# A Mamba and local-attention kernel: dt\*x\*B on GpSimd, scan states in PSUM, a fifth matmul bank, and P times V in one stretch

## The chip, the cores and the metric

The kernel runs on one core of a Trainium2 chip. The metric is the device time of one execution in microseconds. A core has TensorE (PE in the profile; its weight loads are listed as PEld), VectorE (DVE), ScalarE (ACT), GpSimd (POOL) and SyncE (SP), which here only issues DMAs. Each engine works through its own queue in order, and engines wait for each other through semaphores.

## The reference

The input x has 4096 tokens of 256 features. It is normalized once, and two independent branches work on the result:

```python
xn = _layernorm(x)
x  = x + mamba(xn) + local_transformer(xn)
```

The Mamba branch has 512 channels and 16 states per channel. After an input projection, a causal convolution of 4 taps and a silu, it computes dt, B and C for each token and runs the recurrence

```python
dA  = exp(dt * A)                 # per channel and state
h   = dA * h + (dt * x_conv) * B  # along the 4096 tokens
y   = sum over states of h * C
out = (y + x_conv * D) * silu(z) @ out_proj
```

The transformer branch has two layers. Each has 8 heads of 64, with normalized and rotated queries and keys, a softmax over a window of 128 tokens and the window before it, an output projection, and a gated MLP with 682 hidden units. All arithmetic is float32.

## The kernel before, in words

The transformer branch is cut into 16 steps of 256 tokens per layer, so 32 steps `(l, s)`; each step has two attention windows of 128 tokens. The Mamba branch is cut into 8 blocks of 512 tokens, each with 4 groups of 128 channels (`c`). The two branches run interleaved over the whole execution.

The order of the work is not written by hand. Functions such as `project`, `attend`, `mlp`, `prepare` and `recur` only record pieces of work with `add(engine, us, emit, reads, writes, soon=...)`. `Plan.order` (L175 to L281) then lays them out: it keeps a planned time for each engine, takes from the pieces that are ready and whose buffers are free the one with the smallest key, and emits all pieces in the order of their planned starts. The key is the step in which the piece was recorded less its `soon`; `AHEAD` (L43) limits how far ahead of the oldest open piece the plan looks. The numbers `us` and `soon` so decide each engine's queue, and the chip then runs the queues as they stand. A buffer (`buffer(name, n, shape)`) has n tiles that pieces of work take in turn; a new value can be written when all readers of the old one are done.

PSUM has 8 banks of 512 floats per partition. They are: four matmul banks `mm` (L320), one for `dtx` (L321), two for the decays `da` (L322) and one for the sums `y` (L323).

**The recurrence** (`recur`, L709 to L768). For each block, channel group and pair of states `g` (8 pairs): SP loads B and C of the pair, spread over all partitions, into two `bc` tiles (L718 to L723). VectorE multiplies dt\*x (in PSUM, `dtx`) by B into `u` (L726, 128x1024). For each of the two states ScalarE writes the decay exp(dt\*A) into a `da` bank (L734) and VectorE runs the scan along the 512 tokens, reading `da` and `u` and writing the states over `u` (L739). ScalarE copies the last column of both states for the next block (L745). GpSimd multiplies `u` by C (L748, 128x1024), and in every second pair also adds the two states (L753). TensorE adds the result to `y` by transposing matmuls (L757), 4 for an added pair and 8 otherwise. `close` (L770) copies `y` out, transposes it back (L778) and multiplies by the gate.

**The attention** (`project` L836, `attend` L924). TensorE projects q, k, v (L846); ScalarE squares and VectorE reduces for the norms (L857, L859), VectorE and GpSimd rotate (L891, L893, L906, L913, L873), TensorE transposes (L878) and ScalarE copies to `qT`, `kT` (L884). In `attend` each window has two groups `g` of four heads. The scores (L945) use half of the array's rows, 64 x 128. VectorE masks and takes the maximum (L960), ScalarE takes exponentials and divides (L970, L981). TensorE transposes P for two heads at a time (L993), ScalarE copies it to `prT` (L997), and TensorE multiplies it by V (L1005), with half of the array's columns, 128 x 64. Transposing and P times V are recorded separately for each of the two head pairs of a group, the copy between them. `project_out` (L1019, L1028) follows, and `mlp` (L1045) with its up products (L1092) and down products (L1158, L1177).

Each of these products takes a bank of `mm`, which is free again when VectorE or ScalarE has read it out. The float32 matmuls appear as two records each in the profile, the transposes as one.

Of the kernel before, what the change touches and what calls it, by code (L numbers as in the profile page):

```python
# [27 lines left out]
P = 128  # L28
# [3 lines left out]
TB = 512  # L32
# [10 lines left out]
AHEAD = 2.960000  # L43
# [78 lines left out]
class Work:  # L122


    def __init__(self, engine, us, emit, key, late, port):
        self.engine, self.us, self.emit, self.key, self.late, self.port = engine, us, emit, key, late, port
        self.before, self.after, self.values = {}, [], []
        self.n_before = 0
        self.ready = self.start = self.end = 0.0


class Plan:
# [17 lines left out]
    def add(self, engine, us, emit, reads=(), writes=(), late=0.0, port=False, holds=(), soon=0.0):  # L150
# [4 lines left out]
        w = Work(engine, us, emit, self.key - soon, late, port)  # L155
# [19 lines left out]
    def order(self):  # L175
# [3 lines left out]
        port = {"DVE": 0.0, "POOL": 0.0}  # L179
        rank = {w: i for i, w in enumerate(self.works)}  # L180
# [15 lines left out]
        while len(done) < len(self.works):  # L196
# [23 lines left out]
            while open_[e]:  # L220
# [14 lines left out]
                if w.port and e == "DVE" and port["POOL"] > now and chosen is None:  # L235

                    later.append((k, r, w))
                    if len(later) < 4:
                        continue
                    break  # L240
                chosen = w
# [9 lines left out]
            if e == "POOL":  # L251
                start = max(start, port["DVE"])
            elif w.port:
                start = max(start, port["POOL"])
            w.start, w.end = start, start + w.us + self.TAIL[e] + w.late
# [33 lines left out]
def mamba_and_local_transformer(  # L289
# [30 lines left out]
    banks = buffer("mm", 4, [P, 512], psum, True)  # L320
    dtxs_b = buffer("dtx", 1, [P, TB], psum)  # L321
# [9 lines left out]
    queries = buffer("qT", 3, [P, HP, P])  # L331
# [3 lines left out]
    probs_T = buffer("prT", 2, [P, 2, 2, P])  # L335
    heads_T = buffer("OT", 3, [P, HP, P])
# [12 lines left out]
    dts_b = buffer("dt", 2, [P, TB])  # L349
    spreads = buffer("bc", 3, [P, NG, TB])  # L350
# [73 lines left out]
    def dma(kb, to, of, reads=(), writes=(), soon=0.0):  # L424

        add("SP", 0.1, lambda: nc.sync.dma_start(to(), of()), reads, writes, late=2.2 + kb / 170.0, soon=soon)

    def load_qkv(l):
        for s in range(3):
            cut = slice(s * INNER, (s + 1) * INNER)  # L430
            dma(
                512, lambda cut=cut: wqkv.ap[:, :, cut],
                lambda cut=cut: wqkv_d[l][:, cut].rearrange("(k p) n -> p k n", p=P), writes=[(wqkv, s)], soon=-0.85,
            )

    def load_rest(l):
        dma(512, lambda: wo.ap, lambda: wo_d[l].rearrange("(h p) n -> p h n", p=P), writes=[wo], soon=-0.09)
        for half in range(2):
            for m, n in ((0, WHOLE), (NM - 1, LAST)):
# [4 lines left out]
                    writes=[(w1, (half, m))], soon=0.84,  # L444
# [4 lines left out]
            lambda: w2_d[l][0:whole, :].rearrange("(m p) n -> p m n", p=MC), writes=[(w2, 0)], soon=0.33,  # L449
        )  # L450
        dma(112, lambda: w2.ap[0 : HID - whole, NM - 1, :], lambda: w2_d[l][whole:HID, :], writes=[(w2, 1)], soon=1.13)
# [28 lines left out]
        add("PE", 5.3, shift, [w1], [pb], soon=0.05)  # L480
        add("DVE", 0.4, bias, [pb], [b1, b1x])
        add("DVE", 3.2, scale, [], [w1], port=True, soon=-0.08)
# [14 lines left out]
    def base_of(s):  # L497

        base = plan.value(rows_b)
        if s in sums:  # L500
            dma(256, lambda: base.ap, lambda: sums[s].ap, [sums[s]], [base], soon=-1.36)
            return base
        dma(256, lambda: base.ap, lambda: rows(x, s), writes=[base], soon=-1.5)
# [3 lines left out]
            ), [], [base], soon=0.03,  # L507
# [3 lines left out]
    def finish(s, po, base):  # L511

        add("DVE", 0.6, lambda: nc.vector.tensor_tensor(base.ap, halves(po), base.ap, ALU.add), [po], [base], soon=0.27)
        if s in sums:
            dma(256, lambda: rows(out, s), lambda: base.ap, [base], soon=-0.74)
            return
        sums[s] = plan.fixed(dram.tile([P, NW, D], F32, tag=f"sum{s}", name=f"sum{s}"))
        dma(256, lambda: sums[s].ap, lambda: base.ap, [base], [sums[s]], soon=0.48)
# [4 lines left out]
    def shift_column(l, s):  # L523
        now = xts[l, s]
        if s == 0:
            add("POOL", 0.14, lambda: nc.gpsimd.memset(now.ap[:, 1, 0:1], 0.0), [], [(now, 0)], soon=-0.2)
        else:
# [3 lines left out]
                [(old, 1)], [(now, 0)], soon=-0.25,  # L531
            )

    def normalize(s):

        xb, mv, rstd, pt = (plan.value(b) for b in (rows_b, small["mv"], small["rstd"], banks))
        dma(256, lambda: xb.ap, lambda: rows(x, s), writes=[xb], soon=-0.52)
# [26 lines left out]
        add("DVE", 1.1, stats, [xb], [mv], soon=-0.26)  # L564
        add("ACT", 0.5, root, [mv], [rstd], soon=-0.43)
        add("DVE", 0.6, centre, [mv, rstd], [xb], port=True, soon=-0.43)
        now = xts[0, s] = plan.value(tokens)
        add("PE", 0.44, turn, [xb], [pt], holds=[now], soon=-0.59)
        add("ACT", 0.48, lambda: nc.scalar.copy(now.ap[:, :, 1:], halves(pt)), [pt], [(now, 1)], soon=-0.67)
        shift_column(0, s)  # L570
        dma(256, lambda: xn_d[s].ap, lambda: now.ap[:, :, 1:], [(now, 1)], [xn_d[s]], soon=0.02)
# [3 lines left out]
    def reload(s):  # L575
        now = xts[1, s] = plan.value(tokens)
        dma(256, lambda: now.ap[:, :, 1:], lambda: x1_d[s].ap, [x1_d[s]], [(now, 1)], soon=0.49)
# [6 lines left out]
    def in_half(i):  # L584
# [3 lines left out]
            lambda: in_wT[:, i * DI : (i + 1) * DI].rearrange("(k p) n -> p k n", p=P), writes=[w], soon=0.21,  # L588
# [3 lines left out]
    def in_proj(b, w, c, to):  # L592
# [9 lines left out]
        add("PE", 1.72, emit, [w, xms[b]], [pm], holds=[to], soon=0.01)  # L602
        return pm

    def front_load(b):
        xm = xms[b] = plan.value(xms_b)
        for i in range(PB):
            s = b * PB + i
            dma(
                256, lambda i=i: xm.ap[:, :, i * TS : (i + 1) * TS], lambda s=s: xn_d[s].ap, [xn_d[s]], [(xm, i)], soon=0.24  # L610
# [5 lines left out]
    def front_conv(b, c, w):  # L616
        xin, xc, tail = plan.value(rows_m), xcs[b], tails[b]
        edge = slice(c * (TAPS - 1), (c + 1) * (TAPS - 1))
        if b == 0:
            add("POOL", 0.14, lambda: nc.gpsimd.memset(xin.ap[:, 0 : TAPS - 1], 0.0), [], [(xin, 0)], soon=-0.78)  # L620
        else:
# [3 lines left out]
                [(old, c)], [(xin, 0)], soon=-0.2,  # L625
            )
        pm = in_proj(b, w, c, xin)
        add("ACT", 0.48, lambda: nc.scalar.copy(xin.ap[:, TAPS - 1 :], pm.ap), [pm], [(xin, 1)], soon=-0.08)
        if b < NB - 1:
            add(  # L630
                "POOL", 0.14, lambda: nc.gpsimd.tensor_copy(tail.ap[:, edge], xin.ap[:, TB:]), [(xin, 1)], [(tail, c)], soon=0.1
            )
# [4 lines left out]
            ), [], [pm], soon=0.55,  # L637
# [8 lines left out]
        for j in range(TAPS - 1):  # L646
            add("DVE", 0.7, lambda j=j: tap(j), [xin, pm], [(xc, c) if j == TAPS - 2 else pm], soon=0.07)
# [8 lines left out]
    def front_dbl(b):  # L656
# [7 lines left out]
        add("PE", 3.43, emit, [xc], [px], holds=[xd], soon=0.14)  # L664
        add("ACT", 0.48, lambda: nc.scalar.copy(xd.ap, px.ap[0:n]), [px], [xd], soon=0.63)
        xds[b] = xd
        bc = bcs[b] = plan.fixed(dram.tile([2 * NS, TB], F32, tag=f"bc{b}", name=f"bc{b}"))
        dma(64, lambda: bc.ap, lambda: xd.ap[DTR:, :], [xd], [bc], soon=-0.06)

    def gate_conv(b, c, w):  # L670
# [4 lines left out]
        add("ACT", 0.48, lambda: nc.scalar.copy(sz.ap[:, c, :], pz.ap), [pz], [(sz, c)], soon=-1.07)  # L675

    def prepare(b, c):
# [5 lines left out]
            "PE", 1.05, lambda: nc.tensor.matmul(  # L683
                pd.ap, lhsT=dtw[:, c * P : (c + 1) * P], rhs=xd.ap[0:DTR, :], start=True, stop=True
            ), [xd], [pd], holds=[dt, e], soon=0.18,
# [3 lines left out]
        add("ACT", 0.59, lambda: nc.scalar.activation(e.ap[:, n], pd.ap, AF.Abs, bias=col("dt_b", c)), [pd], [e], soon=-1.5)  # L689
        add(  # L690
            "DVE", 0.66, lambda: nc.vector.tensor_scalar(dt.ap, pd.ap, col("dt_b", c), 0.0, ALU.add, ALU.max),
            [pd], [dt],
        )
        add("ACT", 0.54, lambda: nc.scalar.activation(e.ap[:, n], e.ap[:, n], AF.Exp, scale=-1.0), [], [e], soon=0.17)
        add(
            "DVE", 0.36, lambda: nc.vector.tensor_scalar(r.ap[:, n], e.ap[:, n], 1.0, -1.0, ALU.add, ALU.add),
            [e], [r], port=True, soon=-0.9,
        )
        add("POOL", 1.22, lambda: nc.gpsimd.tensor_tensor(r.ap[:, n], e.ap[:, n], r.ap[:, n], ALU.subtract), [e], [r], soon=0.21)
        add("ACT", 0.6, lambda: nc.scalar.activation(e.ap[:, n], e.ap[:, n], AF.Ln, bias=one_t), [], [e], soon=0.1)  # L700
        add("POOL", 1.22, lambda: nc.gpsimd.tensor_tensor(dt.ap, dt.ap, r.ap[:, n], ALU.add), [r], [dt], soon=-0.72)
        add("POOL", 1.22, lambda: nc.gpsimd.tensor_tensor(dt.ap, dt.ap, e.ap[:, n], ALU.add), [e], [dt], soon=-1.32)
        add(
            "DVE", 0.61, lambda: nc.vector.tensor_tensor(dtx.ap, dt.ap, xc.ap[:, c, :], ALU.mult),
            [dt, (xc, c)], [dtx], port=True, soon=-0.87,
# [3 lines left out]
    def recur(b, c, g):  # L709
# [6 lines left out]
        for s in range(2):  # L716
# [4 lines left out]
                .rearrange("n t -> (n t)").partition_broadcast(P), [bc], [w], soon=0.15,  # L721
# [4 lines left out]
            "DVE", 1.15, lambda: nc.vector.tensor_tensor(  # L726
                u.ap, dtx.ap.unsqueeze(1).to_broadcast([P, NG, TB]), spread[0].ap, ALU.mult
            ), [dtx, spread[0]], [u], soon=-0.61,
        )
        for i in range(NG):  # L730
            n = g * NG + i
            da = plan.value(decays)
            add(
                "ACT", 0.63, lambda da=da, n=n: nc.scalar.activation(  # L734
                    da.ap, dt.ap, AF.Exp, scale=negA[:, c * NS + n : c * NS + n + 1]
                ), [dt], [da], soon=0.25,
            )
            add(
                "DVE", 1.18, lambda da=da, n=n, i=i: nc.vector.tensor_tensor_scan(  # L739
                    u.ap[:, i, :], da.ap, u.ap[:, i, :], state.ap[:, c, n : n + 1] if b else 0.0, ALU.mult, ALU.add  # L740
                ), [da, (state, (c, n))], [(u, i)], soon=-1.19,
            )
        if b < NB - 1:
            add(
                "ACT", 0.1, lambda: nc.scalar.copy(state.ap[:, c, g * NG : (g + 1) * NG], u.ap[:, :, TB - 1]),  # L745
                [u], [(state, (c, g * NG + j)) for j in range(NG)], soon=1.05,
            )
        add("POOL", 2.35, lambda: nc.gpsimd.tensor_tensor(u.ap, u.ap, spread[1].ap, ALU.mult), [spread[1]], [u], soon=0.11)  # L748
# [582 lines left out]
```

## Time and profile before

| what | value |
|---|---|
| median of 3 runs | 2031.23 us (2031.15 to 2041.06) |
| profiled execution | 2037.66 us |
| its span | 2035.9 us |
| granted TensorE clock, mean of the span | 0.991 |
| idle time in the span: PE, DVE, ACT, POOL | 108, 311, 401, 626 us |
| DMA | 334.62 MB, 164 GB/s, 49% of 16 engines' time |

The span runs from the first instruction to the last in the profiled execution; the execution's own time is 1.8 us longer. In a row of the groups, the name after the line and engine tells the operation, then what it writes and reads with shapes, how often it ran, the busy time, the mean duration in ns, and behind the second bar the idle time of the engine just before it with what ended most of it. These two rows belong to steps that the change touches:

```profile
L745 ACT COPY state<-u 128x2 f32<-128x2 f32 x224 | 43.4, 194 | 39.2 <-DVE u L739 37.7
L997 ACT COPY prT<-mm 128x512 f32<-128x512 f32 (+1 forms) x256 | 137.6, 578 | 58.7 <-PE mm L993 57.4
```

The first is the copy of the last states: 224 of them, 194 ns each, and ScalarE stood still 39 us before them. The second is the copy of transposed P, for which ScalarE stood 59 us.

### The profile page before, as it was taken

To read this page: it belongs to the slowest core of one execution; us is meant where nothing else is said; L and a number is where in the kernel's file an instruction comes from. 1 tells how busy PE (TensorE), PEld (TensorE's weight loads), DVE (VectorE), ACT (ScalarE), POOL (GpSimd) and SP (SyncE) were. 2 spreads that over 40 slices of the span, in tenths; PEclk is the share of its full clock that TensorE was granted. 3 is DMA by queue.
4 is the path that set the end of the run, shared out by engine and by line. 5 is a ranking of instruction groups with operands and counts; after the bars stand their busy time and mean duration, and the time that the engine had idled before them with its cause. 6 is when DMAs were issued, how large, how long until landed. Compare 5 with 4: busy or idle time off the path is not lost.

```text
span 2035.9 us, 34992 instructions
## 1 busy us (share of the span) xinstructions
PE 1927.6 (95%) x12176; PEld 1411.2 (69%) x12176; DVE 1725.2 (85%) x3022; ACT 1635.3 (80%) x3722; POOL 1410.0 (69%) x1178
## 2 busy tenths in 40 slices
PE   6989999999999999999999999999999999999987
PEld 4566777766777577776768767677676767677776
DVE  5799888999879979798886988979888888888883
ACT  3888888888787888878977888878887878887872
POOL 2676787767667567776775777766687666778762
PEclk9999999999999999999999999999999999999998
DMA  5444554435544345544666444554544644544542
GB/s 167 150 168 162 163 186 164 167 132 185 180 149 164 127 155 182 190 157 143 206 194 207 163 145 143 187 197 150 175 148 158 200 159 156 174 164 158 166 163 72
DMA packets 133922, 334.62 MB, mean 164 GB/s; under 512 B 13452, under 2 KB 57184, under 8 KB 133744
## 3 DMA queue, kind: packets, MB, share of 16 engines
q1 hardware_dynamic: 132752, 331.92, 49.1%
q8 instruction: 96, 1.57, 0.3%
q10 hardware_dynamic: 992, 0.46, 0.1%
q14 instruction: 82, 0.67, 0.1%
HBM read 315.03 MB, written 17.30 MB: 163 GB/s over the span
## 4 chain that ended last, share of the span: by engine, by line
PE 61%; DVE 15%; ACT 11%; DMA 7%; issue 3%; POOL 3%; SPq 0%; DVEq 0%; ACTq 0%; POOLq 0%
PE mm L1092 13%; PE mm L846 9%; PE y L757 5%; DMA bc<-bc 5%; PE mm L1005 5%; DVE u L739 4%; PE mm L945 4%; PE mm L598 4%; PE mm L993 4%; PE mm L1177 3%; PE mm L1028 3%; DVE u L726 3%; PE mm L807 2%; PE mm L1158 2%; PE mm L878 2%
## 5 line engine op out<-in xcount | busy, mean ns | idle before, releaser
L748 POOL TENSOR_TENSOR u<-u,bc 128x1024 f32<-128x1024 f32 x256 | 605.7, 2370 | 295.8 <-ACT state L745 249.7
L739 DVE TENSOR_TENSOR_SCAN u<-da,state,u 128x512 f32<-128x512 f32 x448 | 560.2, 1271 | 27.9 <-ACT da L734 23.3
L734 ACT ACTIVATE da<-dt,negA 128x512 f32<-128x512 f32 x512 | 349.6, 690 | 72.2 <-DVE u L739 70.5
L846 PE MATMUL mm<-wqkv,xt 128*128 128x512 f32 x768 | 363.0, 603 | 13.9 <-DVE turn L891 4.7
L1092 PE MATMUL mm<-hn,w 128*128 128x256 f32 (+1 forms) x1408 | 343.0, 390 | 16.0 <-DVE hn L1083 5.0
L726 DVE TENSOR_TENSOR u<-dtx,bc 128x1024 f32<-128x1024 f32 x256 | 310.6, 1214 | 54.8 <-DMA bc<-bc 41.8
L1092 PEld LDWEIGHTS mm<-hn,w 128*128 128x128 f32 (+1 forms) x1408 | 257.6, 191 | 80.6 <-issue 11.7
L970 ACT ACTIVATE pr<-pr,top 128x256 f32<-128x256 f32 (+1 forms) x512 | 251.5, 494 | 23.0 <-DVE top L960 22.7
L757 PE MATMUL y<-ident,u 128*128 128x128 f32 x1536 | 223.9, 278 | 10.5 <-POOL u L748 5.5
L846 PEld LDWEIGHTS mm<-wqkv,xt 128*128 128x128 f32 x768 | 135.7, 191 | 140.7 <-issue 111.0
L960 DVE CUSTOM_DVE_ANT_0 pr<-mm,maskf,nrm 128x256 f32<-128x256 f32 (+1 forms) x512 | 213.9, 473 | 12.1 <-PE mm L945 11.9
L981 ACT ACTIVATE pr<-pr,den 128x256 f32<-128x256 f32 (+1 forms) x512 | 219.1, 495 | 4.2 <-DVE den L976 3.8
L757 PEld LDWEIGHTS y<-ident,u 128*128 128x128 f32 x1536 | 178.4, 142 | 52.8 <-issue 19.9
L913 POOL TENSOR_TENSOR turn<-turn,trig 128x512 f32<-128x512 f32 x128 | 160.8, 1278 | 67.7 <-DVE turn L906 55.7
L873 POOL TENSOR_TENSOR turn<-turn,turn 128x512 f32<-128x512 f32 x128 | 164.1, 1282 | 49.0 <-DVE turn L891 39.5
L997 ACT COPY prT<-mm 128x512 f32<-128x512 f32 (+1 forms) x256 | 137.6, 578 | 58.7 <-PE mm L993 57.4
L753 POOL TENSOR_TENSOR u<-u 128x512 f32<-128x512 f32 x128 | 162.8, 1273 | 3.8
L945 PEld LDWEIGHTS mm<-kT,qT 64*128 64x128 f32 x2016 | 128.7, 190 | 47.9 <-issue 17.5
L1005 PE MATMUL mm<-prT,v 128*64 128x128 f32 x2016 | 152.6, 285 | 7.5 <-ACT prT L997 7.2
L945 PE MATMUL mm<-kT,qT 64*128 64x128 f32 x2016 | 153.3, 288 | 5.4 <-ACT kT L884 1.8
L993 PE MATMUL mm<-ident,pr 128*128 128x128 f32 x1008 | 142.5, 280 | 10.4 <-ACT prT L997 3.5
L1005 PEld LDWEIGHTS mm<-prT,v 128*64 128x64 f32 x2016 | 112.5, 137 | 55.6 <-ACT prT L997 23.5
(127 smaller groups left out, 3350.3 us busy)
## 6 DMA issues: line engine op xcount, KB each, us to landing
bc<-bc SPq DMA_DIRECT2D x512, 512.0 KB, 4.1
io<-in_x SPq DMA_DIRECT2D x32, 256.0 KB, 4.3
mw<-in_in_wT SPq DMA_DIRECT2D x16, 512.0 KB, 3.9
rot<-in_rot SPq DMA_DIRECT2D x32, 128.0 KB, 3.5
xn<-xt SPq DMA_DIRECT2D x16, 256.0 KB, 3.2
xm<-xn SPq DMA_DIRECT2D x16, 256.0 KB, 4.9
x<-mid SPq DMA_DIRECT2D x16, 256.0 KB, 2.8
mw<-in_out_wT SPq DMA_DIRECT2D x8, 512.0 KB, 4.5
```

The costliest lines, as they stand in the source:

```text
L726: "DVE", 1.15, lambda: nc.vector.tensor_tensor(u.ap, dtx.ap.unsqueeze(1).to_broadcast([P, NG, TB]), spread[0].ap, ALU.mult), [dtx, spread[ ...
L734: "ACT", 0.63, lambda da=da, n=n: nc.scalar.activation(da.ap, dt.ap, AF.Exp, scale=negA[:, c * NS + n : c * NS + n + 1]), [dt], [da], soon ...
L739: "DVE", 1.18, lambda da=da, n=n, i=i: nc.vector.tensor_tensor_scan(u.ap[:, i, :], da.ap, u.ap[:, i, :], state.ap[:, c, n : n + 1] if b el ...
L748: add("POOL", 2.35, lambda: nc.gpsimd.tensor_tensor(u.ap, u.ap, spread[1].ap, ALU.mult), [spread[1]], [u], soon=0.11)
L757: nc.tensor.matmul(y.ap[:, t, :], lhsT=u.ap[:, i, t * P : (t + 1) * P], rhs=ident, is_transpose=True, start=g == 0 and i == 0 and t == 0, ...
L846: nc.tensor.matmul(pm.ap, lhsT=hT[k], rhs=wqkv.ap[:, k, q * INNER : (q + 1) * INNER], start=k == 0, stop=k == KC - 1,)
L945: nc.tensor.matmul(halves(scs[j])[:, i, a * WIN : (a + 1) * WIN], lhsT=qT.ap[half, 2 * g + i, :], rhs=kk.ap[half, 2 * g + i, :], start=n == 0,
L970: nc.scalar.activation(prs[j].ap[:, i, keys], prs[j].ap[:, i, keys], AF.Exp, bias=top.ap[:, h : h + 1], scale=-1.0, accum_out=den.ap[:, h ...
L981: nc.scalar.activation(prs[j].ap[:, i, keys], prs[j].ap[:, i, keys], AF.Copy, scale=den.ap[:, h : h + 1])
L993: nc.tensor.transpose(ppv()[:, j, a, :], prs[j].ap[:, i, a * WIN : (a + 1) * WIN], ident)
L1005: nc.tensor.matmul(hpair(po.ap)[j * DH : (j + 1) * DH, hp, :], lhsT=vv.ap[:, h * DH : (h + 1) * DH], rhs=prT.ap[:, j, a, :], start=a == first,
L1092: nc.tensor.matmul(halves(pm)[0:r, i, :], lhsT=w1.ap[:, k, c0 : c0 + r], rhs=hn.ap[:, k, :], start=k == 0, stop=k == KC - 1,)
```

## The change

1. In `recur`, GpSimd forms dt\*x\*B (which VectorE did), the scan writes the states over the decay in its PSUM bank instead of over `u`, and VectorE multiplies them by C from there, one state at a time, into `u` (which GpSimd did for both at once). The state copy is one for each state instead of one for a pair, and reads the PSUM bank. The sums on TensorE wait for their own state's half of `u`, where they are not added first.
2. `dtx` moves from PSUM to SBUF, and its bank becomes a fifth bank of `mm`.
3. In `attend`, P times V of both head pairs of a group is one piece of work, recorded after both transposes. `prT` has 4 tiles instead of 2; `qT` and `OT` have 2 instead of 3.
4. Pieces of work on TensorE can carry a `part`: "rows" for the scores, "columns" for P times V, nothing for the rest. The planner counts 0.1 us where the part changes, and prefers a piece of the current part to one whose key is up to 0.3 earlier.
5. `AHEAD` goes from 2.96 to 2.7, nearly every `soon` has a new value, the planner's DMA estimate becomes 2.4 us + kb/150 instead of 2.2 us + kb/170, and four of its matmul estimates change a little.

The diff's core; the lines that only have a new `soon` are left out:

```diff
-AHEAD = 2.960000
+AHEAD = 2.700000
+NEAR = 0.3
+SWITCH = 0.1
...
+                if e == "PE" and w.part != part:
+                    later.append((k, r, w))
+                    if k < later[0][0] + NEAR and len(later) < 4:
+                        continue
+                    break
+                if later and e == "PE" and k >= later[0][0] + NEAR:
+                    heappush(open_[e], (k, r, w))
+                    break
...
+            if e == "PE":
+                start += SWITCH * (w.part != part)
+                part = w.part
...
-    banks = buffer("mm", 4, [P, 512], psum, True)
-    dtxs_b = buffer("dtx", 1, [P, TB], psum)
+    banks = buffer("mm", 5, [P, 512], psum, True)
...
-    queries = buffer("qT", 3, [P, HP, P])
+    queries = buffer("qT", 2, [P, HP, P])
...
-    probs_T = buffer("prT", 2, [P, 2, 2, P])
-    heads_T = buffer("OT", 3, [P, HP, P])
+    probs_T = buffer("prT", 4, [P, 2, 2, P])
+    heads_T = buffer("OT", 2, [P, HP, P])
...
+    dtxs_b = buffer("dtx", 1, [P, TB])
...
         add(
-            "DVE", 1.15, lambda: nc.vector.tensor_tensor(
+            "POOL", 2.35, lambda: nc.gpsimd.tensor_tensor(
                 u.ap, dtx.ap.unsqueeze(1).to_broadcast([P, NG, TB]), spread[0].ap, ALU.mult
-            ), [dtx, spread[0]], [u], soon=-0.61,
+            ), [dtx, spread[0]], [u], soon=0.93,
         )
...
-                    u.ap[:, i, :], da.ap, u.ap[:, i, :], state.ap[:, c, n : n + 1] if b else 0.0, ALU.mult, ALU.add
-                ), [da, (state, (c, n))], [(u, i)], soon=-1.19,
+                    h.ap, h.ap, u.ap[:, i, :], state.ap[:, c, n : n + 1] if b else 0.0, ALU.mult, ALU.add
+                ), [(u, i), (state, (c, n))], [h], soon=-0.59,
             )
-        if b < NB - 1:
+            if b < NB - 1:
+                add(
+                    "ACT", 0.1, lambda h=h, n=n: nc.scalar.copy(state.ap[:, c, n : n + 1], h.ap[:, TB - 1 : TB]),
+                    [h], [(state, (c, n))], soon=0.08,
+                )
             add(
-                "ACT", 0.1, lambda: nc.scalar.copy(state.ap[:, c, g * NG : (g + 1) * NG], u.ap[:, :, TB - 1]),
-                [u], [(state, (c, g * NG + j)) for j in range(NG)], soon=1.05,
+                "DVE", 0.61, lambda h=h, i=i: nc.vector.tensor_tensor(
+                    u.ap[:, i, :], h.ap, spread[1].ap[:, i, :], ALU.mult
+                ), [h, spread[1]], [(u, i)], soon=0.15,
             )
-        add("POOL", 2.35, lambda: nc.gpsimd.tensor_tensor(u.ap, u.ap, spread[1].ap, ALU.mult), [spread[1]], [u], soon=0.11)
...
-            add("PE", 0.44, lambda i=i: collect(i), [u], [y], soon=0.16)
+            add("PE", 0.44, lambda i=i: collect(i), [(u, i)], [y], soon=0.0)
...
+            prTs = []
             for i in range(2):
-                hp = 2 * g + i
...
-                def mix(hp=hp, prT=prT):
+                prTs.append(prT)
+
+            def mix():
+                for i, prT in enumerate(prTs):
+                    hp = 2 * g + i
...
-                add("PE", 0.44, mix, [prT] + [vv for _, _, vv in pieces], [(po, hp)], holds=[] if hp else [OT], soon=0.81)
+            add(
+                "PE", 0.93, mix, prTs + [vv for _, _, vv in pieces], [(po, g)], holds=[] if g else [OT], soon=-0.57,
+                part="columns",
+            )
```

## The prediction

> **What bounds the kernel now.** I read the page's busy rows first, then the chain, then the costliest groups, and after that TensorE's waits and its timeline.
>
> ```profile
> span 2035.9 us, 34992 instructions
> ...
> PE 1927.6 (95%) x12176; PEld 1411.2 (69%) x12176; DVE 1725.2 (85%) x3022; ACT 1635.3 (80%) x3722; POOL 1410.0 (69%) x1178
> ...
> PE   6989999999999999999999999999999999999987
> ...
> PE 61%; DVE 15%; ACT 11%; DMA 7%; issue 3%; POOL 3%; SPq 0%; DVEq 0%; ACTq 0%; POOLq 0%
> ...
> L748 POOL TENSOR_TENSOR u<-u,bc 128x1024 f32<-128x1024 f32 x256 | 605.7, 2370 | 295.8 <-ACT state L745 249.7
> L739 DVE TENSOR_TENSOR_SCAN u<-da,state,u 128x512 f32<-128x512 f32 x448 | 560.2, 1271 | 27.9 <-ACT da L734 23.3
> L734 ACT ACTIVATE da<-dt,negA 128x512 f32<-128x512 f32 x512 | 349.6, 690 | 72.2 <-DVE u L739 70.5
> ...
> L726 DVE TENSOR_TENSOR u<-dtx,bc 128x1024 f32<-128x1024 f32 x256 | 310.6, 1214 | 54.8 <-DMA bc<-bc 41.8
> ```
>
> TensorE is full from the second slice to the last but one, and the chain lies on it for 61%. DVE (311 us idle) and ACT (401 us) are second and third. The chain's other 39% are places where TensorE waits for one of them. So the end is TensorE's work plus its waits. Its idle time is 2035.9 - 1927.6 = 108 us, in many small pieces:
>
> ```profile
> PE mm L560 <- DVE io L552: 12.0, 2, 8.9
> PE mm L1005 <- ACT prT L997: 7.2, 13, 0.9
> PE y L757 <- POOL u L748: 5.5, 5, 1.6
> ...
> PE mm L846 <- DVE turn L891: 4.7, 4, 1.5
> PE mm L1092 <- DVE turn L906: 4.4, 7, 1.1
> PE mm L846 <- ACT prT L997: 4.4, 4, 1.2
> ```
>
> Columns: total us, times, longest. L560 is the start. L1005 (P times V) and L757 (y) wait for data. The last three wait for something that isn't their operand: L846 and L1092 write into a bank of `mm` that DVE or ACT has just read out. I sorted all rows of this answer in that way: about 45 us wait for a bank, about 44 us for data (12 of them at the start), and the rest is under 150 ns each.
>
> Busy hides a second loss. The timeline's start times (first column) show what a stretch costs:
>
> ```profile
> 1014.34 1.15 PE L1005 MATMUL mm<-prT,v 128*64 128x128 f32 x16
> 1015.42 1.13 PE L1092 MATMUL mm<-hn,w 128*128 128x256 f32 x4
> ...
> 1026.62 0.66 PE L1005 MATMUL mm<-prT,v 128*64 128x128 f32 x8
> ```
>
> Sixteen records take 1.08 us to the next start. Eight take 0.60 us (medians over the trace 1.075 and 0.595), so two short stretches cost 0.115 us more than one long one. Also, a transpose of y (L757) is followed after 109 ns where the next matmul has the full shape (211 cases), and after 202 ns where it uses half the rows or columns (79 cases): a change of shape costs 93 ns. The first full matmul after P times V takes 57 ns more (166 against 109).
>
> **Part 1: TensorE's work.** No matmul is added or removed. What moves is the order. I counted the built instruction order of both kernels. Stretches of P times V: 164 before, 112 after. Entries from a full shape into a smaller one: 283 before, 205 after (many P times V now follow the scores directly). Exits from P times V to the full shape: 147 and 110. Score stretches: 117 and 114 (two of 1.09 against one of 2.00, 0.18 each).
> 78 x 0.093 = 7.3; 52 x 0.115 = 6.0; 37 x 0.057 = 2.1; 3 x 0.18 = 0.5. Together **-16 us**, all on the bound engine.
> [...] I take the row's 93 ns.
>
> **Part 2: the fifth bank.** `dtx` leaves PSUM and its bank goes to `mm`. From the same order, with each matmul at its measured start-to-start time, I measured how much TensorE work lies between the last write to a bank's old contents and the first write of the new: the median rises from 3.6 to 4.5 us, and reuses closer than 2 us (accumulations aside) fall from about 190 to 112, by 41%. A reader needs a matmul's tail, its queue, and 0.58 (L997) to 0.68 us (L891), so it is the close ones that wait. 41% of 45 us: **-18 us**. Lower bound 0 (the next wait in line takes over), upper 45.
>
> **Part 3: P times V of a group at once, four prT buffers.** Before, 107 of 256 stretches started within 1.2 us of work after their transposes, after it 18 of 128. The 7.2 us wait mostly goes: **-6**. The scores-to-transposes distance is unchanged (median 13.4 and 13.9 us). `qT` and `OT` lose a buffer each; the planner, which keeps the queue in order, must now put an output projection before the next step's first P times V. I put that at nothing, between 0 and +5.
>
> **Part 4: the scan.** GpSimd loses the product with C (256 x 2.37) and gains dt\*x\*B of the same size, both operands in SBUF as before: 0 of 1410 us. What goes is its 249.7 us of blocked queue at L748, behind which the rotary sums stood that L878 waits for (4.1 us): **-3**, between 0 and -10.
> DVE loses 256 x 1.214 = 310.6 and gains 512 products 128x512 with one operand in PSUM. The nearest rows are L891, L893, L906: 682, 684, 677 ns. 512 x 0.68 = 348: +38. The scan now writes PSUM. [...] But this trace has the pair: L641 reads PSUM and writes PSUM in 750 ns (64 times) and SBUF in 746 (32 times): 512 x 0.004 = 2 us. I take the row. DVE becomes 1725 + 40 = 1765 us. Against it, its queue no longer stands 41.8 us at L726 for the DMA of B: GpSimd, with 626 us idle, takes that wait. The product with C waits for a load that went out before. So DVE's blocked and busy time is about level.
> ACT: 448 single-column copies of state instead of 224 (L745, 194 ns): +43 us, 1635 to 1678. As the copies wait for the scan (37.7 us in all before), twice as many wait up to 38 us more, with exponentials and prT copies queued behind. The exponential waits longer as well: its PSUM buffer is held through scan and product, 0.68 us longer. L734's 70.5 us were 85 waits, 0.83 us each; if each grows by 0.68, +58 us on ACT. Its 401 us of idle cover 43 + 38 + 58 = 139, but readers of banks come later. Price on TensorE: ACT and DVE are at 82% and 87% instead of 80% and 85%; scaling queueing by busy/(1-busy), waits grow by 15 to 20%, on the 65 that stay: **+11**. From 0 to +40.
> SP issues the same 512 loads; only who waits for them moves.
>
> **Part 5: new offsets, a shorter horizon (2.96 to 2.70).** They rearrange all queues; their effect on order is already in the counts. TensorE's short waits under 150 ns, which busy hides, are what is left: 1927.6 minus 1837.5 (all matmuls at measured start-to-start times, shape changes included) is 90 us, of which modelled tails before about 95 visible waits are some 14. With fewer close reuses I take a tenth off: **-8**, from +10 to -30.
>
> Sum: -16 - 18 - 6 - 3 + 11 - 8 = **-40 us**. The profiled execution took 2037.7 (span 2035.9); it becomes 1998. The median of the three runs, 2031.2, is 6.4 lower; I forecast against it: **1991 us**.
>
> **Rivals.**
> A, only the shapes count: waits are set by ACT and DVE, whose queues are fuller, so a removed wait comes back elsewhere. For it: the chain's 39% on other engines. Against it: bank waits are real and the spacing changed. 2031 - 16 = 2015.
> B, the order also removes half of the waits: 108 visible and 76 hidden, less 15 at start and end, is 169; half is 85. 2031 - 16 - 85 = 1930, with ACT's copies at +10 still 1940. For it: GpSimd's and DVE's blocked queues go. Against it: DVE at 87% and ACT at 82% would be at 92% and 86% of so short a span.
> C, slower: the decay buffers. There are two; each now waits for exponential, scan, copy and product in turn, and ACT's queue is in order. If a third of the 512 exponentials wait the extra 0.87 us (product and copy), that is 148 us on ACT beside the 43: 1678 + 148, and 330 us of its other waits, make 2156, of which perhaps 100 overlap: about 2055. It decides from about 150 us of idle before the exponentials (72 now). Against it: in the built order the product stands right behind its scan, or one instruction later, in 394 of 512 cases, so the hold mostly grows by 0.68 us alone.
> D, multiplying from PSUM costs far more than 0.68 us: at 0.9, +113 us on DVE, 1875, still under TensorE's; about 2020. This is in A's range.
>
> **Numbers.** Main case 0.49 (1970 to 2008), A with D 0.24 (2008 to 2026), B 0.17 (1930 to 1970), C 0.10 (2030 to 2080). Leaving out C and half of B gives the range 1950 to 2026. A measurement here can tell about 0.5%, 10 us: same is 2021 to 2041. Faster: main, B and two thirds of A, 0.81; same 0.10; slower 0.09.
>
> **What would show it.** TensorE busy near 1900 in a span near 1995; about 112 stretches of P times V; L997's wait at P times V under 3 us; bank waits near 27 us; scan 1270 to 1280 ns and the product 680 ns; DVE near 1765, ACT near 1680 us; the idle before the exponentials under 130 us; no wait of GpSimd for the state copy. I am wrong if scan or product is over 10% longer, if ACT's idle before the exponentials passes 150 us, or if TensorE's idle time stays at 108.

## The result and the profile after

The changed kernel takes 2027.99 us (median of 20 runs, 2022.03 to 2032.82) against 2032.13 (20 runs), a ratio of 0.9977 with a 95% interval of 0.9966 to 0.9988: about 4 us faster. Forecast were 1991 us and a range of 1950 to 2026. The profiled execution took 2028.7 us.

These lines of its page answer to those of before: engine totals, the chain by engine, and the rows of the recurrence.

```profile
span 2027.0 us, 35362 instructions
...
PE 1919.2 (95%) x12176; PEld 1420.8 (70%) x12176; DVE 1766.2 (87%) x3278; ACT 1642.2 (81%) x3946; POOL 1406.8 (69%) x1178
...
DVE 39%; PE 29%; ACT 14%; POOL 7%; issue 6%; DMA 4%; SPq 0%; ACTq 0%; DVEq 0%; POOLq 0%
...
L744 POOL TENSOR_TENSOR u<-dtx,bc 128x1024 f32<-128x1024 f32 x256 | 605.4, 2365 | 202.1 <-PE y L780 76.7
L758 DVE TENSOR_TENSOR_SCAN da<-da,state,u 128x512 f32<-128x512 f32 x448 | 574.7, 1283 | 60.4 <-POOL u L744 45.7
L753 ACT ACTIVATE da<-dt,negA 128x512 f32<-128x512 f32 x512 | 352.0, 692 | 49.6 <-DVE u L768 45.3
...
L768 DVE TENSOR_TENSOR u<-da,bc 128x512 f32<-128x512 f32 x512 | 352.3, 688 | 16.9 <-DMA bc<-bc 3.5
...
L764 ACT COPY state<-da 128x1 f32<-128x1 f32 x448 | 70.2, 164 | 134.7 <-DVE u L768 115.6
```

TensorE is as full as before, 95%, and it stands idle as long as before: 2027.0 - 1919.2 = 107.8 us. The prediction had named just this ("if TensorE's idle time stays at 108") as a sign of being wrong. Yet the chain has moved: 29% of it lies on TensorE (61% before), 39% on VectorE (15%). Most durations are near the forecast (scan 1283 ns, product 688, VectorE 1766 us); ScalarE is busy for 1642 us, not 1680. The last row is the surprise: ScalarE stands 135 us before the state copies, against 39 us in the kernel before. It waits mostly for L768, the product, although the copy only needs the scan. Copy and product read the same PSUM bank. Paired in order, none of the 448 copies overlaps with its product in the trace: 116 end before it begins, 332 start after its end, and the 155 that waited for it start a median 33 ns after it.

TensorE's own list of waits:

```profile
PE mm L901 <- POOL turn L896: 12.4, 17, 2.2
PE mm L801 <- ACT m2k L797: 9.8, 3, 5.1
PE mm L578 <- DVE io L570: 9.5, 1, 9.5
PE mm L1087 <- POOL sq L1095: 8.3, 8, 3.2
PE mm L1087 <- POOL sq L1103: 7.1, 8, 2.2
...
PE mm L1032 <- ACT prT L1020: 2.7, 3, 1.3
```

P times V (L1032) waits 2.7 us for prT, 7.2 before, and no bank wait is among the first eight. At the top stand operands now: rotated queries and keys from GpSimd (L901), the sums for the MLP's mean (L1087), the copied y (L801). Sorted by one rule (data when the releaser wrote an operand of the matmul, bank otherwise), the full lists give 53 us of bank waits and 48 of data waits before, 27 and 72 after. (The prediction's 45 and 44 left small rows out.)

I also split each span by TensorE's start times: nominal work (each matmul at its measured start-to-start time, shape changes included), waits beyond it, and the excess of matmuls in windows in which the granted clock was 0.5. How much counts as nominal depends on how the usual time of a matmul is taken (the prediction had 1837.5 us for the kernel before), so the differences say more than the sums.

| us | before | after | change |
|---|---|---|---|
| nominal work | 1847.6 | 1831.7 | -15.9 |
| waits | 155.7 | 154.2 | -1.5 |
| half clock | 14.5 | 23.4 | +8.9 |
| start, end and rest | 18.0 | 17.7 | -0.3 |
| span | 2035.8 | 2027.0 | -8.8 |

The nominal work fell by the 16 us that were forecast. The waits did not move, and the slower clock took back more than half. Each column is one execution: that of the kernel before was 5.5 us above the median of its 20, that of the changed kernel 0.7 us. If this difference lies in the waits, they rose by about 3 us between typical executions (an estimate: 8.8 - 4.1 - 1.5). The clock's part is steady: the mean granted clock was 0.982 to 0.989 in the 20 executions of the changed kernel, and 0.987 to 0.995 in 76 of the kernel before.

### The profile page after: what moved, and what is told of

Read it like the earlier page. It is cut to its first block, busy times and chain, and to the rows that moved or that the text cites. A ratio compares the mean times of both kernels' runs of the same rounds, so it can differ in the third digit from the quotient of the medians.

```text
span 2027.0 us, 35362 instructions
## 1 busy us (share of the span) xinstructions
PE 1919.2 (95%) x12176; PEld 1420.8 (70%) x12176; DVE 1766.2 (87%) x3278; ACT 1642.2 (81%) x3946; POOL 1406.8 (69%) x1178
## 4 chain that ended last, share of the span: by engine, by line
DVE 39%; PE 29%; ACT 14%; POOL 7%; issue 6%; DMA 4%; SPq 0%; ACTq 0%; DVEq 0%; POOLq 0%
DVE da L758 13%; DVE u L768 7%; PE mm L1122 5%; DVE pr L983 4%; PE mm L869 4%; POOL u L744 3%; DMA bc<-bc 3%; PE mm L968 3%; DVE nrm L882 2%; PE y L780 2%; PE mm L616 2%; PE mm L1207 2%; ACT da L753 2%; PE mm L1032 2%; ACT sq L880 2%
## 5 line engine op out<-in xcount | busy, mean ns | idle before, releaser
L744 POOL TENSOR_TENSOR u<-dtx,bc 128x1024 f32<-128x1024 f32 x256 | 605.4, 2365 | 202.1 <-PE y L780 76.7
L758 DVE TENSOR_TENSOR_SCAN da<-da,state,u 128x512 f32<-128x512 f32 x448 | 574.7, 1283 | 60.4 <-POOL u L744 45.7
L768 DVE TENSOR_TENSOR u<-da,bc 128x512 f32<-128x512 f32 x512 | 352.3, 688 | 16.9 <-DMA bc<-bc 3.5
L1122 PE MATMUL mm<-hn,w 128*128 128x256 f32 (+1 forms) x1408 | 338.1, 388 | 7.4 <-DVE hn L1113 4.1
L780 PE MATMUL y<-ident,u 128*128 128x128 f32 x1536 | 219.3, 276 | 9.5 <-POOL u L776 6.3
L983 DVE CUSTOM_DVE_ANT_0 pr<-mm,maskf,nrm 128x256 f32<-128x256 f32 (+1 forms) x512 | 212.6, 474 | 14.5 <-PE mm L968 11.0
L1004 ACT ACTIVATE pr<-pr,den 128x256 f32<-128x256 f32 (+1 forms) x512 | 224.2, 498 | 1.2 <-DVE den L999 1.2
L764 ACT COPY state<-da 128x1 f32<-128x1 f32 x448 | 70.2, 164 | 134.7 <-DVE u L768 115.6
L968 PE MATMUL mm<-kT,qT 64*128 64x128 f32 x2016 | 160.4, 290 | 5.6 <-ACT kT L907 2.3
L968 PEld LDWEIGHTS mm<-kT,qT 64*128 64x128 f32 x2016 | 133.6, 191 | 45.5 <-issue 15.1
L1032 PE MATMUL mm<-prT,v 128*64 128x128 f32 x2016 | 140.9, 281 | 3.0 <-ACT prT L1020 2.7
```

The costliest lines, as they stand in the source:

```text
L744: "POOL", 2.35, lambda: nc.gpsimd.tensor_tensor(u.ap, dtx.ap.unsqueeze(1).to_broadcast([P, NG, TB]), spread[0].ap, ALU.mult), [dtx, spread ...
L758: "DVE", 1.18, lambda h=h, n=n, i=i: nc.vector.tensor_tensor_scan(h.ap, h.ap, u.ap[:, i, :], state.ap[:, c, n : n + 1] if b else 0.0, ALU. ...
L768: "DVE", 0.61, lambda h=h, i=i: nc.vector.tensor_tensor(u.ap[:, i, :], h.ap, spread[1].ap[:, i, :], ALU.mult), [h, spread[1]], [(u, i)], s ...
L780: nc.tensor.matmul(y.ap[:, t, :], lhsT=u.ap[:, i, t * P : (t + 1) * P], rhs=ident, is_transpose=True, start=g == 0 and i == 0 and t == 0, ...
L968: nc.tensor.matmul(halves(scs[j])[:, i, a * WIN : (a + 1) * WIN], lhsT=qT.ap[half, 2 * g + i, :], rhs=kk.ap[half, 2 * g + i, :], start=n == 0,
L983: nc.vector.tensor_tensor_reduce(out=prs[j].ap[:, i, keys], in0=halves(scs[j])[:, i, keys], in1=mask[:, keys], scale=nrm.ap[:, h : h + 1], ...
```

## The experiments

**Parts one by one, with the plan redone.** Four kernels have one part of the change, or all but one. The diff shows the core of each edit. The expectations weigh two theories. In the coupling theory a wait that is removed on TensorE comes back because other engines are fuller; in the order theory it counts how well the offsets fit the structure.

```diff
b_shapes (on before):  NEAR, SWITCH and parts as in the change; P times V of a group in one piece; prT 4, qT 2, OT 2
b_bank   (on before):
-    banks = buffer("mm", 4, [P, 512], psum, True)
-    dtxs_b = buffer("dtx", 1, [P, TB], psum)
+    banks = buffer("mm", 5, [P, 512], psum, True)
+    dtxs_b = buffer("dtx", 1, [P, TB])
b_scan   (on before):  recur as in the change; dtx in SBUF; four banks
a_4banks (on after):
-    banks = buffer("mm", 5, [P, 512], psum, True)
+    banks = buffer("mm", 4, [P, 512], psum, True)
```

> The kernel before with P times V in one stretch and the planner's rule for parts alone (its buffers prT 4, qT 2, OT 2 with it; old scan, four banks, old offsets and horizon). Coupling theory (a removed wait comes back because VectorE and ScalarE are fuller in the changed kernel): here neither is fuller, so the 16 us of shape changes come through, about 2016 us, and TensorE's waits stay near 156 us or fall by some 6. Order theory (what counts is how well the offsets fit the structure): the old offsets don't fit, waits rise by over 15 us and the time is at 2032 or above, although TensorE's nominal work falls by about 10 to 16.

> The kernel before with the fifth bank alone (dtx in SBUF; the product with B on VectorE then reads two SBUF operands). Coupling theory: bank waits fall and VectorE is no fuller, so TensorE's waits fall by 10 to 18 us: about 2017 us. Order theory: the queue is rearranged by the plan without gain, waits within 10 us of 156, time 2022 to 2045. If the product with B gets slower with both operands in SBUF (over 1.25 us against 1.214) or GpSimd is held up, the difference is named.

> The kernel before with the new scan alone (product with B on GpSimd, states in PSUM, product with C on VectorE, its recorded offsets taken from the changed kernel; four banks, old P times V). Coupling theory: VectorE plus 40 us and ScalarE plus 27 us of copies cost TensorE 10 to 25 us of waits: 2042 to 2057 us. Order theory: the mix of new and old offsets costs more, over 2060 us, with waits spread over all lines.

> The changed kernel with four banks instead of five, nothing else. Coupling theory: the fifth bank is worth what its close reuses cost, 10 to 18 us: 2038 to 2046 us, and bank waits come back to about 45 us in TensorE's list. Order theory: the offsets were fitted to five banks, so over 2050 us. If the bank is worth nothing: 2023 to 2033 us.

| kernel | median us | ratio to before (95%) | nominal | waits | half clock |
|---|---|---|---|---|---|
| b_shapes | 2128.2 | 1.0462 (1.0438 to 1.0485) | 1831.5 | 235.8 | 46.9 |
| b_bank | 2223.8 | 1.0924 (1.0899 to 1.0950) | 1844.2 | 288.3 | 71.1 |
| b_scan | 2129.2 | 1.0468 (1.0450 to 1.0487) | 1849.0 | 217.1 | 48.2 |
| a_4banks | 2123.2 | 1.0436 (1.0420 to 1.0451) | 1832.2 | 227.9 | 44.3 |

All four lose 4 to 9%, by waits and by time at half clock, though b_shapes has the same 16 us less of nominal work. In all four the planner lays out all queues anew with offsets that were chosen for another structure, and three of them lose some 90 us, more than any part was forecast to be worth. The order theory had expected this for those three. That the misfit of the offsets is the cause is not shown, as no run fitted them anew. So these four can't price the parts. b_bank, which lost 190 us, has a second cause:

```profile
L748 POOL TENSOR_TENSOR u<-u,bc 128x1024 f32<-128x1024 f32 x256 | 631.5, 2471 | 245.5 <-ACT state L745 207.9 <-PE mm L993 7.2 <-DVE u L739 7.1
...
L726 DVE TENSOR_TENSOR u<-dtx,bc 128x1024 f32<-128x1024 f32 x256 | 476.7, 1864 | 78.7 <-DMA bc<-bc 61.9 <-PE y L757 7.0 <-POOL u L753 3.7
...
L726 DVE TENSOR_TENSOR u<-dtx,bc x256: 1194/1658/4965, 72.8 to 2177.0; 128x1024 f32<-128x1024 f32 x128
```

VectorE's product takes 1864 ns on average with both operands in SBUF, 1214 with one in PSUM. The last line has the shortest, the median and the longest. The shortest, 1194 ns, is no slower than with PSUM. The 166 products over 1300 ns all end within 5 ns of 1.08 us after the end of an instruction on GpSimd, which is about what a product takes by itself: they end as if each had begun only when GpSimd's instruction was done. So `dtx` could leave PSUM at this price only together with the move of the product to GpSimd.

**Work taken from one engine, queues as they stand.** What the planner is told stays the same here, so that no instruction changes its place; only the emitted instruction is shorter or left out.

```diff
a_dve, b_dve (a_dve41: 474 for 384):
-   h.ap, h.ap, u.ap[:, i, :], state...
+   h.ap[:, 0:384], h.ap[:, 0:384], u.ap[:, i, 0:384], state...
a_pe, b_pe (up products; the mark for the end of the sum moves with it; a_both: this and the cut to 384):
-   for k in range(KC):
+   for k in range(KC if i == 0 else 1):
```

> The changed kernel with every queue as it stands, but the scan covers 384 of the 512 columns (the last quarter of the states is left out): an estimated 512 x 0.27 us = 137 us less work on VectorE. Coupling theory (VectorE has taken over a good part of the chain: 39% of it, TensorE 29%): the time falls by 45 us or more, to 1983 or below, and TensorE's waits by as much. If TensorE alone sets the end, or if the waits come from how the queues are ordered and not from VectorE's load: it falls by less than 20 us, to 2008 to 2028.

> The kernel before with the same cut of the scan to 384 columns, queues unchanged (the last quarter of the states is left out). The chain of before had 15% on VectorE. Coupling theory: VectorE matters less here than in the changed kernel, a fall of 15 to 35 us, to 2000 to 2017. If the two kernels are coupled alike and the change only altered the order: the same fall as in the changed kernel, within 10 us.

> The changed kernel with queues as they stand, but the second tile of each pair of up products leaves out its second half of the sum (160 matmuls of 0.43 us, 69 us less nominal work on TensorE). Coupling theory: TensorE's queue then waits more for VectorE and ScalarE, and only 20 to 45 us come through: 1983 to 2008. If TensorE alone sets the end: 60 us or more, 1968 or below.

> The kernel before with the same 160 matmuls left out (69 us of TensorE's work; second tile of each pair of up products without the second half of its sum), queues unchanged. Coupling theory: more comes through than in the changed kernel, 45 to 69 us: 1963 to 1988. If both are coupled alike: the same as in the changed kernel within 10 us.

> The changed kernel, queues unchanged, the scan over 474 of 512 columns: about 512 x 0.08 = 41 us less on VectorE, which is what the change had added to it (the last 38 columns of the states are left out). If VectorE's added load is what ate the gain of the shapes, as the cut to 384 columns suggests (28 us for 121): the time falls by 8 to 16 us, to 2012 to 2020. If it is something else (the order, the copies): less than 5 us.

> The changed kernel with both cuts together: 384 of 512 scan columns and 160 up matmuls left out. Alone they gave 28 and 0 us. If VectorE hid what TensorE saved, the two together give clearly more than their sum: 50 us or more, to 1978 or below. If TensorE's queue is held by the order of work and not by VectorE's load: about 28 to 35 us, 1993 to 2000.

The change is in per cent of the kernel before, against the uncut kernel's ratio (1 or 0.9977); 1% is 20.3 us. Each ratio is to runs of the kernel before beside that experiment.

| kernel | work less, us | median us | ratio (95%) | change |
|---|---|---|---|---|
| b_pe | PE 69 | 2022.8 | 0.9951 (0.9929 to 0.9973) | -0.5% |
| a_pe | PE 69 | 2029.0 | 0.9991 (0.9978 to 1.0004) | +0.1% |
| b_dve | DVE 119 | 2017.4 | 0.9930 (0.9915 to 0.9945) | -0.7% |
| a_dve | DVE 113 | 2000.1 | 0.9846 (0.9824 to 0.9868) | -1.3% |
| a_dve41 | DVE 32 | 2019.5 | 0.9946 (0.9928 to 0.9963) | -0.3% |
| a_both | PE 69, DVE 115 | 1982.0 | 0.9769 (0.9750 to 0.9788) | -2.1% |

This is the central finding. 69 us less on an engine that is 95% busy give 10 us before and nothing that can be told from zero after. All expectations were above that: even the coupling theory had 20 to 45 us after and 45 to 69 before. The two kernels differ by about 13 us, not much more than the 10 that were to mean alike. In a_pe the nominal work falls by 69.1 us and the waits rise from 154 to 213. The cut of the scan gave 27 us after, between the 45 of the coupling theory and the 20 of its rival, and 14 before, just under the 15 to 35. With VectorE relieved as well, TensorE's cut counts: both together give 2.1% (42 us, where 50 had been expected), alone they add up to 1.2. The chains of a_pe and a_dve, from their pages:

```profile
DVE 42%; PE 24%; ACT 14%; POOL 9%; issue 7%; DMA 4%; SPq 0%; ACTq 0%; DVEq 0%; POOLq 0%
```

```profile
PE 63%; DVE 13%; ACT 13%; POOL 4%; DMA 4%; issue 3%; SPq 0%; ACTq 0%; DVEq 0%; POOLq 0%
```

With less TensorE work the chain lies on VectorE; with 113 us less on VectorE it goes back to TensorE, and the waits fall to 122 us. One wait shows it by itself, that for the rotated queries and keys, which come from VectorE by way of GpSimd. In order: before, a_pe and a_dve (the changed kernel has 12.4 us, above):

```profile
PE mm L878 <- POOL turn L873: 4.1, 3, 3.1
PE mm L901 <- POOL turn L896: 24.8, 33, 3.4
PE mm L901 <- POOL turn L896: 8.2, 14, 1.8
```

With less work in its own queue TensorE stood twice as long for them; with less on VectorE it stood a third less. The changed kernel stands where VectorE takes over from TensorE. Giving back most of the load it added (a_dve41: 32 of 41 us) brings 6 us, a little under the 8 to 16 expected.

**The state copies.**

```diff
a_nocopy, b_nocopy:  the copy's emit does nothing; state is set to zero once at the start
a_latecopy:  the copy is kept back by bank and emitted just before the next exponential into it
+   "ACT", 0.63, lambda h=h, n=n: (last_of(h), nc.scalar.activation(h.ap, dt.ap, AF.Exp, ...
a_dvecopy:  nc.vector.tensor_copy(state..., h.ap[:, TB - 1 : TB]) right after the scan; none on ScalarE
```

> The changed kernel without the 448 copies of the last states (each block starts from zero states; the planned order is unchanged). In the changed kernel ScalarE spends 70 us on them and stands 135 us before them, mostly for the product on VectorE that reads the same PSUM bank. If that standing held up TensorE (copies of prT and the bank readers queue behind it): the time falls by 15 us or more, to 2013 or below. If ScalarE's slack covers it: under 6 us.

> The kernel before without its 224 state copies (each block starts from zero states): 43 us of work and 39 us of standing on ScalarE go, and GpSimd no longer waits for them. If copies cost both kernels alike: the same fall as in the changed kernel, within 4 us. If the changed kernel pays more for them (twice the copies, three times the standing): a smaller fall here, under half.

> The changed kernel with all 448 state copies kept, but each stands in ScalarE's queue right before the exponential that overwrites its decay bank, which has to wait for the product anyway; all else in the queues as it was. If the standing before the copies (135 us) is what costs: most of the 19 to 22 us of leaving them out comes through, 2008 to 2016. If the copies' own 70 us of work cost: under 5 us, 2023 to 2030.

> The changed kernel with the state copy on VectorE, right after the scan, and not on ScalarE. ScalarE gains what it gained without copies (about 20 us of time); VectorE gets 448 short instructions, an estimated 0.1 us each from the 82 ns of its accumulator reads, 45 us, which at 0.15 to 0.23 us of time for each us (the cuts of the scan) cost 7 to 10: 2014 to 2020. If VectorE's load counted fully: 2045 or more.

| kernel | median us | ratio (95%) | change | stands before copy + exponential, us |
|---|---|---|---|---|
| before | 2032.1 | 1 | | 39 + 72 |
| b_nocopy | 2030.6 | 0.9994 (0.9983 to 1.0005) | -0.1% | 0 + 110 |
| after | 2028.0 | 0.9977 (0.9966 to 0.9988) | | 135 + 50 |
| a_nocopy | 2006.4 | 0.9886 (0.9865 to 0.9908) | -0.9% | 0 + 115 |
| a_latecopy | 2020.3 | 0.9929 (0.9911 to 0.9947) | -0.5% | 72 + 42 |
| a_dvecopy | 2045.3 | 1.0053 (1.0033 to 1.0073) | +0.8% | 0 + 138 |

The copies cost the kernel before nothing that shows and the changed kernel about 18 us. The late copy keeps all 448 and half the loss goes (10 us, between the two expectations), because a copy right before the exponential shares a wait that is there anyway:

```profile
L759 ACT ACTIVATE da<-dt,negA 128x512 f32<-128x512 f32 x512 | 353.8, 692 | 41.5 <-DVE u L774 26.5
...
L770 ACT COPY state<-da 128x1 f32<-128x1 f32 x448 | 69.5, 155 | 72.1 <-DVE u L774 70.8
```

The 135 and 50 us have become 72 and 42. a_nocopy stands about as long as a_latecopy in all (115 and 114 us), most of it moved to the exponentials, and is some 9 us faster. So about half of the cost was the standing; the rest goes only when the copies' own 70 us of work do. a_dvecopy shows the price on VectorE: with ScalarE about as free of work as in a_nocopy, 448 copies of 158 ns cost 15 us beyond the changed kernel and 34 beyond a_nocopy, for 47 us more busy time on VectorE. The 2014 to 2020 I had expected took the price of work removed at the scan. Work added between scan and product cost about three times that for each us; that the place is the reason is not shown.

**VectorE relieved, as a version to keep.** The clamp of the norms (a floor under their squares, L923) is 64 instructions of 128x16. They take 524 ns on average, though half of them take under 0.18 us:

```profile
L923 DVE TENSOR_SCALAR nrm<-nrm x64: 142/175/4502, 30.7 to 1941.7; 128x16 f32<-128x16 f32 x64
```

All 19 that take over 400 ns run beside GpSimd's instructions and end about 30 ns after one of them has ended; the longest outlasts six. Here the clamp is replaced by a small constant that is added to every squared norm, so the arithmetic is not quite the same.

```diff
-   lambda: nc.vector.tensor_scalar_max(nrm.ap, nrm.ap, NORM_MIN**2)
+   lambda: None
-   nc.scalar.activation(nrm.ap, nrm.ap, AF.Ln, scale=65536.0)
+   nc.scalar.activation(nrm.ap, nrm.ap, AF.Ln, scale=65536.0, bias=tiny_t)   # 65536 * NORM_MIN**2
```

> As the late copies, and the clamp of the squared norms (64 short instructions on VectorE, [...]up to 4.5 us each) is replaced by a bias in ScalarE's logarithm. VectorE gets about 25 us back: at 0.15 to 0.23, 4 to 6 us under the late copies alone. If these holds do not matter: within 3 us of them.

> The kernel before with the clamp of the squared norms replaced by a bias in ScalarE's logarithm, queues otherwise unchanged: 64 short instructions less on VectorE (25.7 us in its trace). In the changed kernel with late copies this gave 16 us. If VectorE's queue holds TensorE only in the changed kernel: under 8 us here, 2024 to 2034. If it holds it in both alike: 12 to 20 us, 2012 to 2020.

a_late_noclamp takes 2002.5 us, ratio 0.9852 (0.9829 to 0.9875): 25 us under the changed kernel and 30 under the one before, the fastest version that computes all states and products. The clamp alone is worth 16 us there for 22 us of busy time, where I had expected 4 to 6. In the kernel before it is worth 9 us: 2025.9, ratio 0.9956 (0.9940 to 0.9972), just over the 8 expected of a kernel that VectorE doesn't hold. Together with the cuts of the scan (27 us after, 14 before) this says that VectorE holds TensorE in both, more in the changed one. How much of the clamp's worth is VectorE's load and how much its place is open: ScalarE's logarithm stood 26 us for it in the changed kernel.

## Why the prediction was wrong, point by point

- **"So the end is TensorE's work plus its waits."** The step that failed. As an account it holds, but the prediction took the terms as independent: it booked work saved as time saved ("all on the bound engine") and had waits fall by 24 us in all (-18 - 6 - 3 + 11 - 8). They fell by 1.5. Less work in TensorE's queue became more waiting in it: nothing of 69 us came through after, 10 before. The busy share of 95% and the 61% of the chain didn't tell this. a_pe's cut stands in the up products, the change's saving around P times V; that the 16 us went the same way is inferred.
- **"The chain's other 39% are places where TensorE waits for one of them."** A wrong reading: 39% of the span is about 790 us, and TensorE stood idle for 108. On most of that stretch the end was decided on another engine while TensorE was busy with something else. There a saving on TensorE can't shorten the chain.
- **Shapes, -16.** The size was right (-15.9 of nominal work, which b_shapes shows alone as well). It was booked as 16 us of time. The trace has 252 and 170 entries into smaller shapes, not 283 and 205; the difference is nearly the same.
- **Fifth bank, -18, and prT, -6.** Right in place: bank waits fell by 26 us and the prT wait by 4.5. The prediction priced what the fuller engines add at +11; data waits alone rose by 25. The rival A said this ("a removed wait comes back elsewhere"). It was given 0.24 and 2015 us; its direction was right, and even its 16 us didn't all come.
- **VectorE +40.** Measured +41, scan +12 ns instead of +4. What that costs TensorE was put too low with the +11: giving back 32 us of it brings 6, leaving out the copies 18. The two need not add up.
- **ScalarE.** Its standing before exponentials and copies was put at +96 and measured at +73, but distributed otherwise: before the copies +96 instead of +38, before the exponentials -23 instead of +58. I had overlooked that copy and product read one bank; they ran one after the other in all 448 cases. The copies alone cost 18 us, more than the +11 for everything.
- **GpSimd, -3.** L748's wait for the state copy (249.7 us) cost nothing that shows: without the copies GpSimd still stands 255 us there (b_nocopy) and the time is the same. In its place L744 waits for y on TensorE (76.7) and the DMA of B (75.7), and the scan now waits 45.7 us for L744, about as long as VectorE had waited for that DMA. The adding of the two states, which hardly waited before, stands behind VectorE's product:

```profile
L753 POOL TENSOR_TENSOR u<-u 128x512 f32<-128x512 f32 x128 | 162.8, 1273 | 3.8
...
L776 POOL TENSOR_TENSOR u<-u 128x512 f32<-128x512 f32 x128 | 163.4, 1277 | 90.0 <-DVE u L768 85.4
```

- **The clock** was not in the sum: 38 us of the span ran at half clock before, 56 after, at a cost that grew by 9 us. The half-clock stretches of the two profiled executions last 3.4, 6.8 or 10.2 us. Of the 18 that begin before TensorE's last matmul, 15 follow 3.4 us in which TensorE had stood for 1.1 to 2.8 us in all, one follows 3.4 us without any work, and two follow 3.4 us without a pause. Counted in steps of 3.4 us, 2 us or more of standing were followed by half clock in 11 of 14 cases, 1 to 1.5 us in 4 of 37. The table of replanned kernels goes the same way: 217 to 288 us of waits come with 44 to 71 us lost to half clock. So waits that lay close together often cost twice here.
- **Rival C** named the decay bank with its 2 buffers as the danger, but put it before the exponentials and at a net loss of 24 us. A related hold was there, at the copies, and cost about 18.
- **Rival D** adds up to 1878 us on VectorE, not 1875. That changes nothing: the product took 688 ns, not 900.

Open: what each part is worth with offsets fitted to it. Every replanned kernel lost 4% or more, so neither the fifth bank nor the retuned offsets could be priced alone; a fifth bank with the queues held still wasn't tried. That VectorE's added product caused the new data waits is supported by the cuts (and by a_both, and by the wait for the rotated queries and keys), not shown for every wait: the retuned offsets moved all queues at the same time.

## What to carry to other kernels

An engine at 95% isn't yet the bound: take 3% of its work away with all queues held still, and see whether the time moves, before crediting it with a saving. When several engines are over 80% busy, as here, a saving counts only where the chain still lies after it, and work added to the next engine can cost most of its length (34 of 47 us here). Before moving a value into PSUM, list who reads its bank: in this kernel two engines reading it took turns (all 448 times), and the later one held up the queue behind it (ScalarE stood 135 us before the copies).

## What the runs showed of the hardware that I had not expected

- A product of 128x1024 on VectorE took 1214 ns with one operand in PSUM and 1864 (1194 to 4965) with both in SBUF, while GpSimd's ran 2471 instead of 2370. The slow products ended 1.08 us after an instruction of GpSimd.
- A VectorE instruction of 128x16 took 142 to 4502 ns (median 175), and the 19 over 400 ns ended 29 to 37 ns after an instruction of GpSimd.
- The scan took 1283 ns when it wrote to PSUM and 1271 to SBUF. On TensorE a transpose of y was followed after 202 ns by a matmul of half the rows or columns and after 109 by one of the full shape: 93 ns for the change.
- A single-column copy on ScalarE and a product on VectorE that only read the same PSUM bank ran one after the other in all 448 cases. That the bank by itself forces the turns was not shown: in 402 cases the later one carries a wait for a semaphore of the other engine.
